# A state-space layer's depthwise convolution: diagonal matrices on TensorE in place of part of VectorE's multiply-adds, with a new split of the C products

## The chip, the cores and the metric

The kernel runs on one core of a Trainium2 chip. The metric is the device time of one execution in microseconds (us); lower is better. TensorE (PE) multiplies matrices, VectorE (DVE), ScalarE (ACT) and GpSimd (POOL) work elementwise, and SyncE (SP) issues nearly all DMAs. Each engine runs its own instructions in order.

## What is computed

Two layers act on eight images of 256 channels and 48x48 pixels, which are 2304 tokens each. Layer 0 normalizes the image by groups, projects it, finds for each token the 16 most similar tokens, and adds their softmax-weighted features. Layer 1 normalizes again and runs two Mamba blocks one after the other. The core of a block, with 512 inner channels, 4 taps of the depthwise convolution and 16 states:

```
xz = x @ in_w.T ;  xi, z = split(xz)
xc = silu(cb + sum_k xpad[:, k:k+L, :] * cw[:, k])       # depthwise convolution, 4 taps
dt_r, Bm, Cm = split(xc @ xp_w.T) ;  dt = softplus(dt_r @ dtp_w.T + dtp_b)
h  = h * exp(dt * A) + dt * Bm * xc                       # scan over the tokens, 16 states
y  = sum_states(h * Cm) + xc * D ;  y = (y * silu(z)) @ out_w.T
```

The changed part is the second line, and where the product `h * Cm` (the "C product") is done.

## The kernel before

**Units.** Each image is cut into six chunks of T = 384 tokens, and each chunk passes two blocks (DEPTH = 2), so an image has 12 units and the program 96. The channels lie in four blocks of 128 (DB = 4). A unit's scan has 16 steps of 32 channels, each with four groups of states side by side on 128 partitions; a step has two parts of two states. So a unit has 32 parts, and the program 3072 scans on DVE.

**The main loop** (L991 to L1008) walks over the parts m. In each part ACT makes the decays of the next part (`decay`, L828, two PSUM buffers), DVE runs the scan (`run_scan`, L843), and POOL makes the inputs B·dt·x two steps ahead (`make_bx`, L804). POOL's C products of the step before come once a step (`pool_part`, L871). Which engine does the C product of a part is set by the letters of `SHARE` (L73): "G" gives it to POOL, "V" to DVE (L845). There are three patterns of 16 letters, used for

- stage 0: units 1 to 9 of an image that has a successor. The next image's top-16 search runs beside them, also on DVE;
- stage 1: units 0, 10 and 11 of such an image. The next image's normalization and projections run beside them;
- stage 2: the last image, which has nothing beside it.

**The rest of a unit** is woven into the loop by two hand-written tables, `between` (emitted before the part's scan) and `behind` (after it). An entry such as `(-21, in_proj, 0)` places `in_proj` of channel block 0 in the part 21 before the unit's first scan. After both, one slice of the next image's attention is emitted (`ahead.go`). The schedule is manual: the order of the tables is each engine's order.

**The convolution before.** `in_proj` (L602) writes a block's 387 columns (three of history and 384 tokens) into PSUM. `tap` (L694, ACT) multiplies by the last tap, adds the bias and writes the tile `xc`. `taps` (L702, DVE) adds the three other taps with one multiply-add each, reading PSUM:

```
nc.vector.scalar_tensor_tensor(
    unit["xc"][e], unit["pe"][e][:, k : k + T], cw[:, unit["d"], e, k : k + 1],
    unit["xc"][e], ALU.mult, ALU.add,
)
```

`silu_x` (L710), `x_proj` (L717), `split`, `step_size` (L732) and `softplus` (L741) follow.

**Buffers.** All matmul outputs but the attention sum share a ring of three PSUM buffers (tag `mm`, L559): a matmul can start only when the third tile before it has been read for the last time. The SBUF tag `ow` has one buffer, used in turn by the squares of the normalization (`square`, L643) and the output weights (`load_out`, L900).

**The start.** Layer 0 of the first image runs alone (L524 to L529). After it, eight 128x128 diagonal matrices of the skip weights `D` are made on DVE (L540) and written to HBM (`diag`); `load_d` fetches them for `sum_states` (L886).

Of the kernel before, what the change touches and what calls it, by code (L numbers as in the profile page):

```python
# [8 lines left out]
F32 = mybir.dt.float32  # L9
BF16 = mybir.dt.bfloat16  # L10
AF = mybir.ActivationFunctionType
ALU = mybir.AluOpType
# [3 lines left out]
P = 128  # L16
# [9 lines left out]
def tile_conv_preact(  # L26
# [18 lines left out]
    nc = tc.nc  # L45
    B, C, N = x.shape
    DEPTH, DI, NS = A_log.shape
    DC = conv_w.shape[2]
# [3 lines left out]
    DB = DI // P  # L52
    NB = N // P
    T = 384
# [3 lines left out]
    G = 32  # L58
# [3 lines left out]
    H = DC - 1  # L62
    PARTS = Q // HQ
# [4 lines left out]
    BLOCK = 16  # L68
    TOPK = (1, 10)
# [3 lines left out]
    SHARE = ("GGVGGGVVGGGGGGVG", "GGGVGVVGVVVGVGVG", "VGVGVGVVGGVVGGVG")  # L73
    assert N % T == 0 and N % P == 0 and T % P == 0 and NS % (J * HQ) == 0

    const = ctx.enter_context(tc.tile_pool(name="const", bufs=1))
    small = ctx.enter_context(tc.tile_pool(name="small", bufs=2))
    hbm = ctx.enter_context(tc.tile_pool(name="hbm", bufs=2, space=DRAM))
# [8 lines left out]
    ident = const.tile([P, P], F32, tag="ident", name="ident")  # L87
# [3 lines left out]
    three = const.tile([P, 1], F32, tag="three", name="three")  # L91
    nc.gpsimd.memset(three, 3.0)
    tiny = const.tile([P, 2], F32, tag="tiny", name="tiny")
# [4 lines left out]
    ones_col = const.tile([P, 1], F32, tag="ones_col", name="ones_col")  # L98
    nc.gpsimd.memset(ones_col, 1.0)
    eps5 = const.tile([P, 1], F32, tag="eps5", name="eps5")  # L100
# [29 lines left out]
    cw = const.tile([P, DEPTH, DB, DC], F32, tag="cw", name="cw")  # L130
    cbias = const.tile([P, DEPTH, DB], F32, tag="cbias", name="cbias")
    dtb = const.tile([P, DEPTH, DB], F32, tag="dtb", name="dtb")
    dpar = const.tile([P, DEPTH, DB], F32, tag="dpar", name="dpar")
# [389 lines left out]

    lefts = [{} for _ in range(B)]  # L524
    with tc.tile_pool(name="first", bufs=1) as pool0, tc.tile_pool(
        name="first_ps", bufs=1, space=PSUM
# [5 lines left out]

    diag = hbm.tile([P, DEPTH, DC + 1, DB, P], F32, tag="diag", name="diag", bufs=1)
    with tc.tile_pool(name="setup", bufs=2) as setup:
        for d in range(DEPTH):
            for t in range(DC, DC + 1):
                dg = setup.tile([P, DB, P], F32, tag="dg", name=f"dg_{d}_{t}")
                for k in range(DB):
                    f = cw[:, d, k, t : t + 1] if t < DC else dpar[:, d, k : k + 1]
                    nc.vector.tensor_scalar(dg[:, k], ident, f, None, ALU.mult)  # L540
                nc.sync.dma_start(diag[:, d, t], dg)

    keep = ctx.enter_context(tc.tile_pool(name="keep", bufs=2))
# [14 lines left out]
    def mm(w, name):  # L558
        return ps.tile([P, 512], F32, tag="mm", name=name, bufs=3)[:, :w]  # L559
# [127 lines left out]
    def load_d(unit, k):  # L687
        unit["dmat"][k] = keep.tile([P, P], F32, tag="dmat", name=f"dmat_{unit['u']}_{k}")
        nc.sync.dma_start(unit["dmat"][k], diag[:, unit["d"], DC, k])

    def tap(unit, e):
        d = unit["d"]
        o = keep.tile([P, T], F32, tag="xc", name=f"xc_{unit['u']}_{e}", bufs=7)
        nc.scalar.activation(  # L694
            o, unit["pe"][e][:, H:], AF.Identity,
            bias=cbias[:, d, e : e + 1], scale=cw[:, d, e, H : H + 1],
        )
        unit["xc"][e] = o

    def taps(unit, e):  # L700
        for k in range(H):
            nc.vector.scalar_tensor_tensor(  # L702
                unit["xc"][e], unit["pe"][e][:, k : k + T], cw[:, unit["d"], e, k : k + 1],
                unit["xc"][e], ALU.mult, ALU.add,
            )
# [86 lines left out]
    def on_pool(unit, i, p):  # L792

        stage = 2 if unit["b"] + 1 == B else 0 if TOPK[0] <= unit["at"] < TOPK[1] else 1
        return SHARE[stage][(i * PARTS + p) % BLOCK] == "G"

# [115 lines left out]
    def leave(unit, cb):  # L912
# [17 lines left out]
        (-35, center), (7, in_proj, 5), (24, sum_states, 2), (-33, variance), (-21, in_proj, 0),  # L930
        (-15, taps, 1), (38, out_proj, 0), (-15, taps, 2), (-14, taps, 3), (-34, square),
        (39, leave, 0), (23, load_rep, "dt", 14), (5, load_rep, "dt", 5), (-4, load_bc, 1), (38, out_proj, 1),
        (17, load_d, 2), (-17, tap, 1), (18, load_rep, "dtx", 13), (-8, times_x, 1), (19, gate, 1),
        (-22, normal), (1, load_rep, "dt", 3), (0, load_rep, "dtx", 4), (15, load_rep, "dt", 10), (6, load_rep, "dtx", 7),
        (10, load_rep, "dtx", 9), (12, load_rep, "dtx", 10), (20, load_rep, "dtx", 14), (11, gate, 0), (-29, spread_root),
        (-19, load_in, 5), (33, load_out), (-22, load_in, 0), (21, load_rep, "dt", 13), (-20, tap, 0),
        (-10, step_size, 1), (9, copy_z, 2), (-18, in_proj, 2), (2, load_rep, "dtx", 5), (10, sum_states, 0),
        (13, load_rep, "dt", 9), (29, gate, 2), (9, silu_z), (7, load_rep, "dt", 6), (19, load_rep, "dt", 12),
        (-6, load_rep, "dtx", 1), (-14, load_in, 7), (-30, root), (9, load_rep, "dt", 7), (4, load_d, 1),
        (-24, load_in, 3), (17, load_rep, "dt", 11), (14, load_rep, "dtx", 11), (-13, x_proj), (-17, load_in, 6),  # L940
        (-3, load_d, 0), (4, load_rep, "dtx", 6), (-4, load_rep, "dtx", 2), (-42, load_v),
    ]
    behind = [
        (-12, split), (-3, load_rep, "dt", 1), (3, in_proj, 4), (-10, step_size, 0), (-5, load_rep, "dt", 0),
        (-8, load_rep, "dtx", 0), (-15, tap, 3), (-1, load_rep, "dt", 2), (-28, scale), (16, load_rep, "dtx", 12),
        (11, load_rep, "dt", 8), (8, in_proj, 6), (17, sum_states, 1), (-14, silu_x), (25, load_rep, "dt", 15),
        (-37, affine), (1, times_x, 2), (7, copy_z, 0), (8, load_rep, "dtx", 8), (-17, tap, 2),
        (-10, softplus), (-16, in_proj, 3), (3, load_rep, "dt", 4), (-29, load_in, 2), (6, in_proj, 7),
        (35, gate, 3), (-2, load_rep, "dtx", 3), (8, copy_z, 1), (40, leave, 1), (-3, times_x, 3),
        (22, load_rep, "dtx", 15), (-16, load_in, 4), (29, load_d, 3), (-37, mean), (-19, taps, 0),  # L950
        (-19, in_proj, 1), (-10, load_bc, 0), (33, sum_states, 3), (-30, root_end), (-9, times_x, 0),
# [39 lines left out]
    for m in range(first, PARTS * NSTEP - HOOKS + last + 1):  # L991
        n, p = divmod(m, PARTS)
# [57 lines left out]
```

## Time and profile before

The time before is 9905.45 us, the median of three runs (9903.67 to 9908.92). The profiled execution spans 9897.1 us. Starts of every 32nd scan in the timeline give the units: the first scan starts at 517.7 us; a unit of stage 0 takes 98.3 us in the mean (63 units), of stage 1 100.5 (21 units), of the last image 89.7 (12 units). The page's first part gives the engines:

| Engine | Busy us | Share of the span | Instructions |
|---|---|---|---|
| PE (matmul) | 8000.3 | 81% | 36736 |
| DVE | 8956.8 | 90% | 7993 |
| ACT | 7322.2 | 74% | 15966 |
| POOL | 8943.3 | 90% | 3927 |

These shares are means over stages with different limits, so they are to be read together with the busy time by stage. A busy matmul row overlaps with its neighbours; its mean duration is not its cost in a stream. The mean granted TensorE clock is 0.889 of full speed, and DMA packets take 44.7% of the 16 DMA engines' time.

### The profile page before, as it was taken

Reading aid. Unit: us, or ns where it says so; the run is one execution under the profiler, and the core shown is the slowest. Engines: PE = TensorE matmul, PEld = TensorE weight load, DVE = VectorE, ACT = ScalarE, POOL = GpSimd, SP = SyncE. Lnnn points to the kernel's source line nnn. Section 1 sums busy time; section 2 is a strip of 40 time slices with the busy share of each in tenths; the row PEclk is TensorE's granted clock in tenths of the full one; section 3 lists DMA queues with packets and bytes.
Section 4 is the critical chain, followed back from the end, with each engine's and each line's share of the span. In section 5 each row is a group of like instructions: output and inputs, shape, how many; then the busy total and the mean of one; then the engine's idle time right before and its main releaser. Section 6 shows DMA issues by size and latency. Waiting matters only on the chain. (4 is left out here: it accounts for less than half of the span.)

```text
span 9897.1 us, 133780 instructions
## 1 busy us (share of the span) xinstructions
PE 8000.3 (81%) x36736; PEld 4388.5 (44%) x36736; DVE 8956.8 (90%) x7993; ACT 7322.2 (74%) x15966; POOL 8943.3 (90%) x3927
## 2 busy tenths in 40 slices
PE   8878887788878888788877888778887788866665
PEld 6644544444534454445444445344544444522222
DVE  4589998999989999899998999899998999988998
ACT  4477777778777877777877787777787778766766
POOL 0099999999989999899998999999998999999999
PEclk9989998899989998899988999889998899977777
DMA  1144445444444444444454444444445444444544
GB/s 32 37 133 126 134 130 152 124 132 129 136 142 131 129 134 137 140 126 133 130 148 128 130 128 134 144 132 125 135 128 152 121 133 127 138 136 129 145 138 122
DMA packets 1243503, 1271.37 MB, mean 128 GB/s; under 512 B 266592, under 2 KB 1215840, under 8 KB 1242752
## 3 DMA queue, kind: packets, MB, share of 16 engines
q1 hardware_dynamic: 1230496, 1262.45, 44.7%
q8 instruction: 293, 4.80, 0.2%
q14 instruction: 458, 3.75, 0.1%
q10 hardware_dynamic: 12256, 0.36, 0.1%
HBM read 1048.94 MB, written 212.86 MB: 127 GB/s over the span
## 5 line engine op out<-in xcount | busy, mean ns | idle before, releaser
L804 POOL TENSOR_TENSOR bx<-BC,dtxr 128x1536 f32<-128x1536 f32 x1536 | 5298.4, 3453 | 115.6 <-PE y L889 59.8
L828 ACT ACTIVATE da<-dtr,A_sb 128x385 f32<-128x385 f32 x6144 | 3591.0, 585 | 871.6 <-DVE bx L843 558.0
L843 DVE TENSOR_TENSOR_SCAN bx<-da,bx 128x770 f32<-128x770 f32 x2040 | 3521.8, 1746 | 190.5 <-ACT da L828 151.4
L871 POOL TENSOR_TENSOR bx<-bx,BC 128x1536 f32<-128x1536 f32 (+1 forms) x1320 | 3303.6, 2503 | 217.5 <-DVE bx L843 205.4
L843 DVE TENSOR_TENSOR_SCAN da<-da,bx 128x770 f32<-128x770 f32 x1032 | 1808.8, 1753 | 193.4 <-ACT da L828 149.0
L602 PE MATMUL pe<-vn,inw 128*128 128x384 f32 (+1 forms) x3072 | 1258.9, 543 | 394.1 <-DVE xr L924 87.0
L399 PE MATMUL psim<-pos 128*128 128x512 f32 (+1 forms) x2880 | 1370.8, 608 | 183.5 <-ACT sim L408 74.7
L465 PE MATMUL po<-feat,aT 128*128 128x256 f32 x5184 | 1364.0, 412 | 13.8 <-ACT aT L454 7.6
L889 PE MATMUL y<-bx,sel 128*32 128x384 f32 x12288 | 1221.2, 533 | 44.2 <-POOL bx L871 37.9
L465 PEld LDWEIGHTS po<-feat,aT 128*128 128x128 f32 x5184 | 1029.8, 205 | 361.9 <-issue 113.9
L845 DVE TENSOR_TENSOR bx<-da,BC 128x768 f32<-128x768 f32 x1032 | 988.8, 958 | 35.5
L602 PEld LDWEIGHTS pe<-vn,inw 128*128 128x128 f32 x3072 | 590.1, 206 | 902.6 <-issue 191.2
L399 PEld LDWEIGHTS psim<-pos 128*128 128x128 f32 x2880 | 552.8, 206 | 818.8 <-issue 470.8
L889 PEld LDWEIGHTS y<-bx,sel 128*32 128x32 f32 x12288 | 394.1, 118 | 856.6 <-issue 725.0
L702 DVE SCALAR_TENSOR_TENSOR xc<-pe,cw,xc 128x384 f32<-128x384 f32 x1152 | 695.7, 611 | 42.8 <-ACT xc L694 15.7
L732 PE MATMUL pd<-dbl,dtp_sb 16*128 16x384 f32 x768 | 424.3, 668 | 342.0 <-ACT dt L741 209.0
L859 ACT COPY h_st<-da 128x2 f32<-128x2 f32 x832 | 131.7, 158 | 686.4 <-DVE bx L845 680.0
L454 ACT ACTIVATE aT<-pt 128x512 f32<-128x512 f32 (+1 forms) x720 | 388.1, 548 | 245.9 <-PE pt L446 239.8
L445 PE MATMUL pt<-ident,sim 128*128 128x128 f32 x2592 | 539.6, 291 | 33.7 <-DVE v L666 17.6
L907 PE MATMUL pw<-z,ow 128*128 128x384 f32 x1536 | 531.5, 499 | 15.0 <-DVE v L666 7.0
L437 ACT ACTIVATE rest<-left,three 128x512 bf16<-128x512 f32 (+1 forms) x720 | 467.0, 670 | 59.7 <-DVE left L422 59.7
L446 PE MATMUL pt<-minus,rest 128*128 128x128 bf16 x2592 | 491.6, 225 | 3.2 <-ACT rest L437 3.2
(146 smaller groups left out, 9766.8 us busy)
## 6 DMA issues: line engine op xcount, KB each, us to landing
dtxr<-dtx_d SPq DMA_DIRECT2D x6144, 48.0 KB, 1.8
dtr<-dt_d SPq DMA_DIRECT2D x6144, 48.0 KB, 1.8
BC<-bc_d SPq DMA_DIRECT2D x768, 192.0 KB, 3.7
inw<-in_in_wT_dram SPq DMA_DIRECT2D x768, 128.0 KB, 2.2
dtx_d<-dtx SPq DMA_DIRECT2D x384, 192.0 KB, 2.0
dt_d<-dt SPq DMA_DIRECT2D x384, 192.0 KB, 2.2
ow<-in_out_wT_dram SPq DMA_DIRECT2D x96, 512.0 KB, 4.0
dmat<-diag SPq DMA_DIRECT2D x384, 64.0 KB, 2.3
```

The source lines that it names most:

```text
L399: nc.tensor.matmul(pm, pos[:, k, t * P : (t + 1) * P], pos[:, k, c0 : c0 + w], start=(k == 0), stop=(k == CB - 1),)
L445: nc.tensor.transpose(pt[:, q], row["sim"][:, r], ident)
L465: nc.tensor.matmul(row["po"], aT[:, m % PT, :], feat[:, m, :], start=(m == 0), stop=(m == NB - 1))
L602: nc.tensor.matmul(pe, w[:, k], unit["vn"][:, k, lo:], start=(k == 0), stop=(k == CB - 1))
L702: nc.vector.scalar_tensor_tensor(unit["xc"][e], unit["pe"][e][:, k : k + T], cw[:, unit["d"], e, k : k + 1], unit["xc"][e], ALU.mult, ALU.add,
L804: nc.gpsimd.tensor_tensor(bx[:, :, 1:], unit["BC"][0], unit["dtxr"][i].unsqueeze(1).to_broadcast([P, Q, T]), ALU.mult,)
L828: nc.scalar.activation(da[:, s * (1 + T) : (s + 1) * (1 + T)], unit["dtr"][i], AF.Exp, scale=A_sb[:, unit["d"], i, p * HQ + s : p * HQ + s ...
L843: nc.vector.tensor_tensor_scan(h, da, g, 0.0, ALU.mult, ALU.add)
L845: nc.vector.tensor_tensor(bx[:, :, 0:T], da.rearrange("p (q t) -> p q t", q=HQ)[:, :, 1:], unit["BC"][1][:, qs], ALU.mult,)
L871: nc.gpsimd.tensor_tensor(g[:, :, 0:T], g[:, :, 1:], unit["BC"][1][:, qs], ALU.mult)
L889: nc.tensor.matmul(y[j * G : (j + 1) * G, :], sel, unit["bx"][k * J + j][:, q, 0:T], start=False, stop=True, skip_group_check=True,)
L907: nc.tensor.matmul(pw, unit["ow"][:, k, cb * P : (cb + 1) * P], unit["z"][k], start=(k == 0), stop=(k == DB - 1),)
```

## The change

For some channel blocks the convolution moves from DVE to PE. A depthwise tap is a product with a diagonal matrix, so four matmuls with the matrices diag(cw[:, k]) against four shifted windows of the block's 387 columns add up the four taps in PSUM. `ON_PE` says for which blocks: 0 and 1 in stage 0, all four in stages 1 and 2. For such a block ACT first copies the 387 columns from PSUM to SBUF (`tap`), PE runs `conv`, and ACT reads the sum back and adds the bias (`drain`); `taps` does nothing. The diagonals, 32 for the taps and 8 for `D`, are made in front of layer 0 of the first image and lie in HBM; `load_taps` fetches those of two blocks (512 KB) into the `ow` buffer.

The time that this frees on DVE goes in part to C products: `SHARE` gives POOL fewer of them, 22 of 32 parts in stage 0 (before 24), 13 of 32 in stages 1 and 2 (before 16). The tables are adapted: `in_proj` of block 1 comes one part earlier, `tap` 1 two parts earlier, `silu_x` and `x_proj` half a part later. Four small constants are put into one tile to save SBUF.

```diff
-    SHARE = ("GGVGGGVVGGGGGGVG", "GGGVGVVGVVVGVGVG", "VGVGVGVVGGVVGGVG")
+    SHARE = ("GGVGGGVVGGGGGGVVGGVGGGVVGGGGGGVV", "GGVVGVVGVVVGVGVGGGVVGVVGVVVGVVVG", "VGVGVGVVGGVVVGVGVGVGVGVVVGVVVGVG")
+    ON_PE = ((0, 1), (0, 1, 2, 3), (0, 1, 2, 3))
...
+    diag = hbm.tile([P, DEPTH, DB, DC + 1, P], F32, tag="diag", name="diag", bufs=1)
+    with tc.tile_pool(name="setup", bufs=2) as setup:
+        for d in range(DEPTH):
+            for k in range(DB):
+                dg = setup.tile([P, DC + 1, P], F32, tag="dg", name=f"dg_{d}_{k}")
+                for t in range(DC + 1):
+                    f = cw[:, d, k, t : t + 1] if t < DC else dpar[:, d, k : k + 1]
+                    nc.vector.tensor_scalar(dg[:, t], ident, f, None, ALU.mult)
+                nc.sync.dma_start(diag[:, d, k], dg)
+
     lefts = [{} for _ in range(B)]
...
     def tap(unit, e):
         d = unit["d"]
-        o = keep.tile([P, T], F32, tag="xc", name=f"xc_{unit['u']}_{e}", bufs=7)
-        nc.scalar.activation(
-            o, unit["pe"][e][:, H:], AF.Identity,
-            bias=cbias[:, d, e : e + 1], scale=cw[:, d, e, H : H + 1],
-        )
-        unit["xc"][e] = o
+        o = keep.tile([P, H + T], F32, tag="xc", name=f"xc_{unit['u']}_{e}", bufs=7)
+        unit["xi"][e], unit["xc"][e] = o, o[:, 0:T]
+        if e in ON_PE[stage(unit)]:
+            nc.scalar.copy(o, unit["pe"][e])
+        else:
+            nc.scalar.activation(
+                o[:, 0:T], unit["pe"][e][:, H:], AF.Identity,
+                bias=cbias[:, d, e : e + 1], scale=cw[:, d, e, H : H + 1],
+            )
...
+    def load_taps(unit, e0):
+        if e0 in ON_PE[stage(unit)]:
+            t = keep.tile([P, DB * C], F32, tag="ow", name=f"cd_{unit['u']}_{e0}", bufs=1)
+            t = t.rearrange("p (e k c) -> p e k c", e=2, k=DC)
+            nc.sync.dma_start(t, diag[:, unit["d"], e0 : e0 + 2, 0:DC])
...
+    def conv(unit, e):
+        if e in ON_PE[stage(unit)]:
+            cv = unit["cv"][e] = mm(T, f"cv_{unit['u']}_{e}")
+            for k in range(DC):
+                nc.tensor.matmul(
+                    cv, unit["taps"][e][:, k], unit["xi"][e][:, k : k + T],
+                    start=(k == 0), stop=(k + 1 == DC),
+                )
+
+    def drain(unit, e):
+        if e in ON_PE[stage(unit)]:
+            nc.scalar.activation(
+                unit["xc"][e], unit["cv"].pop(e), AF.Identity, bias=cbias[:, unit["d"], e : e + 1]
+            )
...
     between = [
+        (-21, in_proj, 0), (-20, tap, 0), (-19, tap, 1), (-18, drain, 0), (-18, in_proj, 2), (-17, drain, 1), (-17, tap, 2),
+        (-15, conv, 2), (-14, conv, 3), (-14, drain, 2), (-13, drain, 3), (-13, silu_x),
...
     behind = [
+        (-20, in_proj, 1), (-19, conv, 0), (-18, conv, 1), (-16, in_proj, 3), (-15, tap, 3), (-25, load_taps, 0),
+        (-17, load_taps, 2), (-13, x_proj), (-12, split), (-3, load_rep, "dt", 1), (3, in_proj, 4), (-10, step_size, 0), (-5, load_rep, "dt", 0),
```

## What the change is predicted to do

> **What bounds the kernel now.** I read the page's first part first: DVE and POOL are both busy 90% of the span, and in the first 440 us POOL has next to nothing to do. So these two come first. The next view is the busy time by stage. I took nine units of stage 0, three of stage 1 and eleven of stage 2 (columns: length; busy us and, in brackets, instructions of PE, PE weight loads, DVE, ACT, POOL; granted clock; DMA share; GB/s):
>
> ```profile
> 1805.00:2688.00 883.00, 762.41 (x3609) 424.23 (x3607) 851.81 (x749) 693.88 (x1519) 864.71 (x323) 0.93 0.46 131
> 2688.00:2991.00 303.00, 222.10 (x986) 118.31 (x985) 257.29 (x241) 216.57 (x473) 266.98 (x171) 0.83 0.49 142
> 8820.00:9806.00 986.00, 606.70 (x2430) 263.91 (x2430) 885.26 (x769) 688.54 (x1516) 921.14 (x384) 0.75 0.48 137
> ```
>
> Per unit, stage 0 is 98.1 us with POOL busy 96.1 (98%) and DVE 94.6 (96%): both are full, and neither alone is the bound. Stage 1 is 101.0 us with POOL 89.0 and DVE 85.8, so some 12 us go to handoffs. Stage 2 is 89.6 us with POOL 83.7 and DVE 80.5. PE fills 86% of stage 0 but 62% of stage 2.
>
> The waits of DVE say what the missing time in stage 2 is (us in total, times, longest):
>
> ```profile
> DVE da L843 <- ACT da L828: 38.1, 17, 3.2
> DVE bx L843 <- ACT da L828: 34.9, 19, 3.1
> ```
>
> That is 6.6 us a unit: a burst on ACT (table load, silu or softplus) makes the next decay late. The same two are 1.4 us a unit in stage 0. The groups by shape give the prices (busy us, mean ns | idle before):
>
> ```profile
> L804 POOL TENSOR_TENSOR bx<-BC,dtxr 128x1536 f32<-128x1536 f32 x1536 | 5298.4, 3453 | 115.6 <-PE y L889 59.8 <-DMA dtxr<-dtx_d 24.6 <-ACT da L828 15.8
> L871 POOL TENSOR_TENSOR bx<-bx,BC 128x1536 f32<-128x1536 f32 x720 | 2292.8, 3184 | 139.2 <-DVE bx L843 131.4 <-DMA xt<-in_x_dram 4.2 <-DVE den L430 2.1
> L871 POOL TENSOR_TENSOR bx<-bx,BC 128x768 f32<-128x768 f32 x600 | 1010.9, 1685 | 78.3 <-DVE bx L843 74.0 <-DMA dtr<-dt_d 3.0 <-DMA dtxr<-dtx_d 0.7
> L845 DVE TENSOR_TENSOR bx<-da,BC 128x768 f32<-128x768 f32 x1032 | 988.8, 958 | 35.5
> L702 DVE SCALAR_TENSOR_TENSOR xc<-pe,cw,xc 128x384 f32<-128x384 f32 x1152 | 695.7, 611 | 42.8 <-ACT xc L694 15.7
> L602 PE MATMUL pe<-vn,inw 128*128 128x387 f32 x1536 | 648.0, 553 | 243.1 <-ACT vn L679 62.8 <-issue 48.6 <-ACT aT L454 30.8
> L907 PE MATMUL pw<-z,ow 128*128 128x384 f32 x1536 | 531.5, 499 | 15.0 <-DVE v L666 7.0 <-DMA ow<-in_out_wT_dram 3.3 <-ACT feat L346 1.3
> L694 ACT ACTIVATE xc<-pe,cbias,cw 128x384 f32<-128x384 f32 x384 | 245.3, 662 | 114.5 <-PE pe L602 114.4
> L337 ACT ACTIVATE pos<-pp,b_pos 128x384 f32<-128x384 f32 x96 | 55.1, 573 | 68.5 <-PE pp L310 68.4
> L761 ACT COPY z<-pe 128x384 f32<-128x384 f32 x288 | 136.7, 475 | 79.2 <-PE pe L602 79.2
> ```
>
> For DVE and PE I use busy over count, since neighbours overlap: a tap costs DVE 695.7/1152 = 0.604 us, and a 384-column matmul in a stream costs PE 0.346 (L907) to 0.422 us (L602), not its 0.5 us of duration.
>
> **What the Trainium skill says.** "Perfetto Trace Analysis", section Identifying the Most-Contended Engine, takes occupancy as a fair measure on Vector and GpSimd and not for matmuls; the trace agrees, as the overlap just used shows. "GPSIMD Engine Reference", section 3.1 Elementwise, gives a two-input fp32 operation on GpSimd 1.96 times its time on Vector; here the 768-wide C product costs 1685 ns against 958, a ratio of 1.76, and I use these. "Perfetto Trace Analysis", section Optimizing Scalar/DVE Operations, warns that the two share an SBUF read port, so that moving work between them may not help; nothing in this trace shows it, as all 1536 POOL products of L804 take 3407 to 3547 ns whatever DVE does. "TensorE: Matmul & The Clock Gate", section Step-by-step, says that weight loads are pulled ahead while the matmuls stay in program order; so a convolution that waits for ACT holds the attention matmuls behind it.
>
> **DVE, part by part.** Blocks on PE: 63 units x 2 + 33 x 4 = 258. Three taps each leave: 774 x 0.604 = -467 us. C products taken from POOL: 63 x 2 + 33 x 3 = 225 x 0.958 = +216 us. Sum -252 us; per unit -3.62 + 1.92 = **-1.71** in stage 0, and -7.25 + 2.87 = **-4.37** in stages 1 and 2.
>
> **POOL.** By the letters, a stage-0 unit loses two products of one part (-3.37 us), a stage-1 unit three (-5.06), a stage-2 unit turns three pairs into single parts (-3 x 1.50 = -4.5). The sum is -372 us. So in stage 0 DVE comes to 92.9 and POOL to 92.7: still level.
>
> **ACT.** Per block a tap of 0.662 becomes a copy of 387 columns, near L761's 0.475, and a drain, near L337's 0.573: +0.386, or +100 us in all, +0.8 a unit in stage 0 and +1.5 elsewhere. ACT is busy 77 of 98 us, and it waits for scans (680 us at L859, 558 at L828 in the whole run), so the busy time itself is hidden. The drain's wait need not be: behind it on ACT stand the next decays, and DVE waits for these. Each drain stands right behind its convolution in the tables (conv 0 after part -19's scan, drain 0 ahead of part -18's). When today's tap waits for its matmul it waits 114.4/73 = 1.57 us. Bounds for the 258 drains are therefore 0 and 405 us of ACT time; as ACT has slack on every part outside its bursts, I take 70 us arriving at DVE.
>
> **PE.** 258 x 4 = 1032 matmuls x 0.346 to 0.422 = +357 to +435 us, about 3.1 us a stage-0 unit: 84.7 becomes 87.8 of some 96 us, 91%. It is hidden if the ring of three PSUM buffers holds. There the change helps: today's projections keep a buffer until DVE's last tap (PE waits 82.4 us for `xc` L702 at the matmul of L886 alone), while on the new path a quick copy frees it. The convolutions add a tile each, emptied one part later.
>
> **DMA.** 63 + 66 = 129 loads of 512 KB, 66 MB on 1271 MB, with 45% of the DMA engines' time in use: hidden. A load of this size takes 4.0 us to land (that of the output weights); blocks 2 and 3 have from the end of part -17 to part -15, some 3 to 5 us, so PE may wait 1 to 2 us there in stages 1 and 2, where over a quarter of its time is free. The `ow` buffer's wait stops the SP queue for part of a part, and the replica loads behind it run one to two steps ahead.
>
> **The start loses.** Before, the image loads go out at once. ACT and DVE there (start us, duration):
>
> ```profile
> 4.82 1.02 DVE L261 BATCH_NORM_STATS2 st<-xs 128x6 f32<-128x384 f32 x2 [4.82 <-DMA xs<-in_x_dram]
> ...
> 27.87 0.23 DVE L155 TENSOR_SCALAR A_sb<-A_sb 128x128 f32<-128x128 f32 x1 [11.58 <-ACT A_sb L153]
> ```
>
> Layer 0's statistics end at 16 us, and ACT takes their mean at 24.0, after its own DMA issues. In the changed program's order, all eight diagonal writes stand ahead of the image loads on SP, which also reuse the space of their tiles; and on DVE the last two sets stand behind L155. So: 28.1 + 10 x 0.28 (L540 took 0.28 each) = 31; the write lands 2.5 later; the load takes 4.0, the statistics 11: they end near 48.6 instead of 16, and the mean comes near 49 instead of 24: +25 us, with nothing beside it. At the end of the lone stage, the old setup held the load of `v` from 442 to 445: -3. Net **+22** (10 to 28).
>
> **The sum.** Stage 0: both full engines lose 1.7 and 3.4, so 63 x 1.71 = -108 if the idle share stays. Stage 1: units that lose 12 us to handoffs won't follow DVE in full; 60% of 21 x 4.37 is -55. Stage 2: 12 x 4.37 = -52, as ACT's bursts stay what they are. New drain waits +70, but POOL's relief and the looser ring give back part of DVE's 3.5 idle us in stage 0, for which I take 1.1 x 63 = -70. With the start +22: -193, hence **9712 us**.
>
> **Rivals.**
> - *PE becomes the bound of stage 0*: at 91% it pays for each added matmul, so stage 0 gains nothing; half of stages 1 and 2 (-72) and the start: 9855. For it speaks PE's 86%; against it, that PE's longest waits there are for ACT.
> - *The drain's wait replaces the taps*: two thirds of 405 us reach DVE, +270, with the same -252 and +22: 9945, slower. For it: the short distance of conv and drain, and 1.4 to 6.6 us a unit that DVE already waits for decays. Against: ACT's waits for scans.
> - *Everything follows*: stage 0 gains POOL's full 3.37, the others 4.37: -212 - 144 + 22 gives 9571.
>
> **How the numbers follow.** The sum as computed 0.60, spread over 9630 to 9810; PE bound 0.14, mostly 9810 to 9900; drain waits 0.13; everything follows 0.13, half of it under 9620. A range of 9620 to 9900 leaves out the drain rival and half of the last, 0.2. Faster by over 0.2% (under 9886): 0.60 + 0.13 + 0.09 = 0.82; within 0.2%: 0.05; slower: 0.13.
>
> **What would show it.** Right: DVE down by some 250 us and POOL by 370 in the first part, PE up by 400; stage-0 units near 96 us, stage 2 near 86; the first statistics about 30 us late. The drain rival would show as ACT waiting over 200 us on the convolution's rows and DVE's waits for L828's decays doubled; the PE rival as PE over 95% in stage 0 with DVE under 93%. I am wrong if DVE's busy time falls as computed and the units don't get shorter.

## The result and the profile after

The changed kernel takes **10558.1 us** (median, 10550.2 to 10569.2) against 9907.0 us of the kernel before (9903.7 to 9908.9) on the same chip: a ratio of 1.0658, 95% interval 1.0640 to 1.0677. The forecast was 9712 us, faster; it was wrong in direction and by 846 us. The profiled execution spans 10550.1 us at a mean granted clock of 0.892 (before 0.889), so the clock is no part of it.

The page's first part, to be read against the table of engines of before:

```profile
PE 8642.9 (82%) x38800; PEld 4798.1 (45%) x38800; DVE 8738.7 (83%) x7476; ACT 7435.5 (70%) x16254; POOL 8590.9 (81%) x3738
```

DVE is busy for 218 us less than before and POOL for 352 us less: the work did leave them. PE is busy for 643 us more. Every share but PE's fell. So no engine became full; all of them wait more.

The busy time by stage (nine units of stage 0, three of stage 1, eleven of the last image; columns as in the prediction):

```profile
1916.00:2860.00 944.00, 821.02 (x3759) 459.87 (x3758) 826.90 (x698) 698.28 (x1528) 830.72 (x303) 0.92 0.45 127
2860.00:3192.00 332.00, 247.19 (x1078) 134.74 (x1079) 257.76 (x230) 226.18 (x496) 259.36 (x165) 0.84 0.49 141
9428.00:10457.00 1029.00, 694.20 (x2788) 321.49 (x2792) 842.41 (x670) 707.95 (x1591) 875.00 (x385) 0.80 0.50 143
```

Per unit of stage 0, DVE is busy 91.9 us (826.90/9; before 94.6) and POOL 92.3 (before 96.1), as forecast, but PE 91.2 (before 84.7), and the unit takes 104.9 us: DVE's idle time went from 3.5 to 13 us.

What DVE waits for, over the whole run (us in total, times, longest). First before:

```profile
DVE bx L843 <- ACT da L828: 151.4, 186, 3.1
DVE da L843 <- ACT da L828: 149.0, 61, 5.7
DVE z L895 <- PE y L889: 117.7, 69, 4.3
...
DVE xr L491 <- PE pr L482: 13.4, 2, 12.3
```

Then after (L843 is now L873, L828 is L858, L895 is L925, L491 is L490):

```profile
DVE bx L873 <- ACT da L858: 386.4, 158, 6.6
DVE da L873 <- ACT da L858: 316.8, 169, 6.5
DVE xr L490 <- PE pr L481: 286.8, 65, 12.3
DVE z L925 <- PE y L919: 275.4, 100, 7.2
```

These four rows hold most of the answer. Scans waiting for decays went from 300 to 703 us: that is ACT being late. The last step of the attention (`xr` waits for the transposed sum `pr`) went from 13 to 287 us, and the gate (`z` waits for `sum_states`) from 118 to 275 us: that is PE being late. POOL feels it too: its next inputs go into buffers that `sum_states` must have read, and they wait for that 287 us in all, against 60 before. The groups by shape give the work that was added and removed (busy us, mean ns | idle before):

```profile
L726 PE MATMUL cv<-xc,cd 128*128 128x384 f32 x2064 | 735.1, 500 | 69.3 <-DMA cd<-diag 54.2 <-ACT xc L698 8.7 <-ACT da L858 5.4
L709 DVE SCALAR_TENSOR_TENSOR xc<-pe,cw,xc 128x384 f32<-128x384 f32 x378 | 230.8, 611 | 16.6 <-ACT xc L700 7.7
L733 ACT ACTIVATE xc<-cv,cbias 128x384 f32<-128x384 f32 x258 | 148.9, 577 | 375.4 <-PE cv L726 375.2
L698 ACT COPY xc<-pe 128x387 f32<-128x387 f32 x258 | 121.8, 472 | 2.9 <-PE pe L601 2.9
```

The first line shows an error of the prediction at sight: the program has 258 x 4 = 1032 convolution matmuls, and the trace has 2064 rows (instructions that the trace lists). The drains wait 375 us for their convolutions.

### The profile page after: what moved, and what is told of

Read it like the earlier page. It is cut to its first block, busy times and chain, and to the rows that moved or that the text cites. A ratio compares the mean times of both kernels' runs of the same rounds, so it can differ in the third digit from the quotient of the medians.

```text
span 10550.1 us, 137600 instructions
## 1 busy us (share of the span) xinstructions
PE 8642.9 (82%) x38800; PEld 4798.1 (45%) x38800; DVE 8738.7 (83%) x7476; ACT 7435.5 (70%) x16254; POOL 8590.9 (81%) x3738
## 4 chain that ended last, share of the span: by engine, by line
DVE 36%; PE 24%; ACT 19%; issue 8%; DMA 6%; SPq 6%; POOL 2%; ACTq 0%; POOLq 0%; DVEq 0%
DVE da L873 11%; DVE bx L873 10%; ACT da L858 7%; PE cv L726 6%; SPq L575 4%; PE pe L601 4%; DVE bx L875 3%; PE po L464 3%; DVE top L414 3%; PE psim L398 3%; DVE left L417 2%; PE y L919 2%; DMA dtxr<-dtx_d 2%; DVE xc L709 2%; PE px L747 1%
## 5 line engine op out<-in xcount | busy, mean ns | idle before, releaser
L858 ACT ACTIVATE da<-dtr,A_sb 128x385 f32<-128x385 f32 x6144 | 3590.9, 585 | 783.4 <-DVE bx L873 437.3
L901 POOL TENSOR_TENSOR bx<-bx,BC 128x768 f32<-128x768 f32 (+1 forms) x1131 | 2928.8, 2590 | 723.1 <-DVE bx L873 444.1
L873 DVE TENSOR_TENSOR_SCAN bx<-da,bx 128x770 f32<-128x770 f32 x1815 | 3134.8, 1747 | 407.4 <-ACT da L858 386.4
L873 DVE TENSOR_TENSOR_SCAN da<-da,bx 128x770 f32<-128x770 f32 x1257 | 2204.3, 1754 | 343.4 <-ACT da L858 316.8
L398 PE MATMUL psim<-pos 128*128 128x512 f32 (+1 forms) x2880 | 1381.7, 617 | 161.7 <-DVE xc L709 104.3
L601 PE MATMUL pe<-vn,inw 128*128 128x384 f32 (+1 forms) x3072 | 1206.5, 523 | 285.2 <-DVE xr L954 88.1
L875 DVE TENSOR_TENSOR bx<-da,BC 128x768 f32<-128x768 f32 x1257 | 1204.3, 958 | 43.2
L919 PE MATMUL y<-bx,sel 128*32 128x384 f32 x12288 | 1178.4, 521 | 26.4 <-DVE bx L875 23.1
L726 PE MATMUL cv<-xc,cd 128*128 128x384 f32 x2064 | 735.1, 500 | 69.3 <-DMA cd<-diag 54.2
L747 PE MATMUL px<-xc,xp_sb 128*48 128x384 f32 x768 | 368.7, 639 | 283.1 <-ACT xc L740 283.1
L762 PE MATMUL pd<-dbl,dtp_sb 16*128 16x384 f32 x768 | 385.6, 618 | 260.6 <-ACT dt L771 211.7
L726 PEld LDWEIGHTS cv<-xc,cd 128*128 128x128 f32 x2064 | 396.8, 195 | 371.6 <-issue 33.0
```

What stands on the lines that cost most here:

```text
L398: nc.tensor.matmul(pm, pos[:, k, t * P : (t + 1) * P], pos[:, k, c0 : c0 + w], start=(k == 0), stop=(k == CB - 1),)
L601: nc.tensor.matmul(pe, w[:, k], unit["vn"][:, k, lo:], start=(k == 0), stop=(k == CB - 1))
L726: nc.tensor.matmul(cv, unit["taps"][e][:, k], unit["xi"][e][:, k : k + T], start=(k == 0), stop=(k + 1 == DC),)
L858: nc.scalar.activation(da[:, s * (1 + T) : (s + 1) * (1 + T)], unit["dtr"][i], AF.Exp, scale=A_sb[:, unit["d"], i, p * HQ + s : p * HQ + s ...
L873: nc.vector.tensor_tensor_scan(h, da, g, 0.0, ALU.mult, ALU.add)
L875: nc.vector.tensor_tensor(bx[:, :, 0:T], da.rearrange("p (q t) -> p q t", q=HQ)[:, :, 1:], unit["BC"][1][:, qs], ALU.mult,)
```

## The experiments

Unit means are taken as for the kernel before, from the starts of every 32nd scan. Every kernel was timed beside the kernel before on the same chip; differences with a plus sign are against that timing of it (medians of 9898 to 9907 us).

| Kernel | us (median) | Ratio (95% interval) | Unit: stage 0 / 1 / last image |
|---|---|---|---|
| before | 9907.0 | 1 | 98.3 / 100.5 / 89.7 |
| the change | 10558.1 | 1.0658 (1.0640 to 1.0677) | 105.6 / 106.4 / 93.5 |
| none_on_pe | 10390.2 | 1.0499 (1.0468 to 1.0529) | 103.3 / 105.7 / 94.4 |
| old_share | 10483.4 | 1.0593 (1.0562 to 1.0623) | 104.3 / 106.4 / 93.6 |
| one_tap | 10174.7 | 1.0281 (1.0245 to 1.0316) | 101.8 / 101.6 / 90.0 |
| pe_load_here | 10143.7 | 1.0249 (1.0220 to 1.0279) | 101.8 / 101.5 / 89.3 |
| pe_load_spread | 10072.8 | 1.0176 (1.0133 to 1.0220) | 100.9 / 101.1 / 89.3 |
| share_only | 10027.8 | 1.0131 (1.0087 to 1.0174) | 99.6 / 101.0 / 92.0 |
| order_only | 10284.9 | 1.0391 (1.0346 to 1.0435) | 102.4 / 104.5 / 92.5 |
| silu_back | 9936.0 | 1.0035 (1.0021 to 1.0050) | 98.8 / 100.2 / 89.7 |
| silu_alone | 9945.0 | 1.0037 (1.0017 to 1.0057) | 98.9 / 100.7 / 89.8 |
| x_proj_later | 10227.2 | 1.0329 (1.0299 to 1.0359) | 102.3 / 102.1 / 92.2 |
| change_silu_back | 10376.0 | 1.0479 (1.0451 to 1.0510) | 102.5 / 105.8 / 96.0 |
| last_image | 10016.4 | 1.0116 (1.0087 to 1.0146) | 98.8 / 100.7 / 96.4 |
| last_once | 9969.4 | 1.0069 (1.0046 to 1.0092) | 98.8 / 100.7 / 92.2 |
| last_once_sum | 9974.1 | 1.0076 (1.0047 to 1.0105) | 99.3 / 101.1 / 89.7 |
| last_two | 9916.8 | 1.0017 (1.0009 to 1.0025) | 98.9 / 100.4 / 88.9 |
| last_two_letters | 9900.3 | 1.0000 (0.9990 to 1.0010) | 98.9 / 100.4 / 87.2 |
| rows_by_image | 9874.0 | 0.9972 (0.9961 to 0.9982) | 98.3 / 101.0 / 87.3 |
| four_by_image | 9889.1 | 0.9987 (0.9980 to 0.9994) | 98.3 / 100.7 / 88.3 |

### Which part of the change costs the time

**none_on_pe** leaves the new rows, letters and setup, with no block on PE:

```diff
-    ON_PE = ((0, 1), (0, 1, 2, 3), (0, 1, 2, 3))
+    ON_PE = ((), (), ())
```

> The changed kernel with no channel block on TensorE: tables, split of the C products and early setup stay, only the convolutions go back to VectorE. Three theories. P (TensorE's queue): the convolution costs TensorE two passes per matmul, 735 us in all, in a stretch where its queue was full, and VectorE waits behind. Then all of the excess but the start's goes, and VectorE, with 216 us of C products more than before, sets the time: 9905 + 23 for the start + 120 to 200, about 10,050 to 10,130 us. H (handoff): the drains' waits on ScalarE delay the decays; the same is expected, 10,050 to 10,130. S (split and order): the new split of the C products and the new order of the tables cost the time; then it stays over 10,400 us.

10390 us, just under the bound of S: still 5% slower than before without a single convolution on PE. So most of the loss needs neither the convolution on PE nor its handoffs.

**old_share** puts the old letters into the changed kernel (`SHARE` as before, the rest as changed).

> The changed kernel with the old split of the C products (24, 16 and 16 of 32 parts on GpSimd). P: stage 0 is set by TensorE and doesn't care, since neither VectorE (2 us less a unit) nor GpSimd (3.4 us more, 96 of 105) is the bound: within 0.7% of 10,558 us. H: VectorE's time still counts beside the waits, so its 216 us less show at least by half: 10,350 to 10,450. S: most of the loss is undone, under 10,250 us.

75 us faster than the change, at the edge of P's range and short of H's. POOL again has its C products and DVE loses 216 us of them: the letters are a smaller part.

**one_tap** keeps copies, loads, drains, letters and rows, and runs one matmul of each convolution's four; three of four taps are left out for those blocks:

```diff
-            for k in range(DC):
+            for k in range(DC - 1, DC):
...
-                    start=(k == 0), stop=(k + 1 == DC),
+                    start=True, stop=True,
```

> The changed kernel with one matmul per block in place of four: three of the four taps are left out on the blocks that TensorE convolves. Copy, wait, drain, loads and order stay, so all handoffs are there; TensorE's added passes fall from 2064 to 516. P: the loss goes nearly whole: VectorE at 93 and GpSimd at 93 us set stage-0 units of 95 to 98 us, and the time is 9,750 to 9,950 us. H: the drains and the waits stay, so most of the loss stays: over 10,300 us.

383 us faster than the change, between the two forecasts, so the amount of work on PE matters, with all handoffs in place. DVE's wait for `pr` falls from 287 to 76 us and that for `sum_states` from 275 to 191.

**order_only** is the work of before in the new order: no block on PE and the old letters, with the new rows and the setup in front.

> The changed kernel with no block on TensorE and the old split of the C products: every engine has the work of the kernel before, only the order of the tables and the early setup are the new ones. The runs so far left 10,390 us with nothing on TensorE, so a fourth theory, O (order), stands beside P and S: the new rows put x_proj on TensorE directly behind silu_x of ScalarE, in front of the part's attention matmuls instead of behind them, and TensorE's whole queue waits there for silu_x. O: 10,150 to 10,330 us. S (split): the order is harmless, 9,910 to 9,980 us.

10285 us: **+382 us from the order and the setup alone**, the largest single part. The letters, added to that, give none_on_pe (+105 us), and the convolution on PE, added to that, the change (+168 us, although it takes 467 us of taps from DVE).

### The row of silu_x

**silu_back** is order_only with two rows, `silu_x` and `x_proj`, put where they were; **silu_alone** moves back `silu_x` only, **x_proj_later** puts `x_proj` half a part later still and leaves `silu_x` in its new place:

```diff
-        (-15, conv, 2), (-14, conv, 3), (-14, drain, 2), (-13, drain, 3), (-13, silu_x),
+        (-15, conv, 2), (-14, conv, 3), (-14, drain, 2), (-13, drain, 3),
...
-        (-17, load_taps, 2), (-13, x_proj), (-12, split), ...
+        (-17, load_taps, 2), (-12, split), ...
...
+        (-13, x_proj)          # in between
+        (-14, silu_x)          # in behind
```

> order_only with silu_x and x_proj put back to their old rows (silu_x behind part -14, x_proj in front of part -13's scan); the other moved rows (in_proj 1, tap 0 to 2 and the place of the rows in their parts) stay. O with silu_x and x_proj as the cause: back to the kernel before plus the start's 10 to 15 us, 9,900 to 9,980. If another moved row is the cause: as order_only, within 60 us.

> order_only (10,285 us) with silu_x alone put back behind part -14; x_proj keeps its new row behind part -13. Two theories of the 349 us between order_only and silu_back. R (ScalarE's own wait): in the old row ScalarE runs the silu burst in time in which it would wait for VectorE's scan of part -14; one part later it first idles there (3.3 us in the last image) and then makes the next decays wait behind the burst. Q (TensorE's queue): x_proj now waits for silu_x with the attention matmuls behind it. R: 9,920 to 9,990 us. Q: with silu_x early, x_proj does not wait either, so the same is expected; the next run tells them apart.

> order_only with x_proj alone half a part later (in front of part -12's scan, behind the attention matmuls of part -13); silu_x keeps its new row. Q: TensorE no longer waits with attention behind it, so most of the 349 us go: under 10,050 us. R: the burst still stands behind ScalarE's wait, and split comes yet closer to x_proj: 10,230 to 10,340 us.

silu_back takes away 349 of the 382 us, silu_alone 340, x_proj_later 58. One row, moved by half a part, costs 3.4% of the run. DVE's waits for decays in order_only:

```profile
DVE bx L873 <- ACT da L858: 374.9, 157, 4.4
DVE da L873 <- ACT da L858: 224.7, 110, 6.7
```

and in silu_back:

```profile
DVE da L873 <- ACT da L858: 147.8, 62, 5.6
DVE bx L873 <- ACT da L858: 142.1, 186, 3.1
```

600 against 290 us: the 310 us are most of the difference in time. The timeline shows how. ACT in silu_back, around part -14 of unit 88 (start us, us, then in brackets the idle time before and what ended it):

```profile
9178.66 1.21 ACT L858 ACTIVATE da<-dtr,A_sb 128x385 f32<-128x385 f32 x2 [3.25 <-DVE bx L873]
9179.89 1.28 ACT L738 ACT_TABLE_LOAD   x1
9181.18 1.76 ACT L740 ACTIVATE xc<-xc 128x384 f32<-128x384 f32 x4
9182.96 1.28 ACT L741 ACT_TABLE_LOAD   x1
9184.25 0.16 ACT L889 COPY h_st<-da 128x2 f32<-128x2 f32 x1
9184.44 1.20 ACT L858 ACTIVATE da<-dtr,A_sb 128x385 f32<-128x385 f32 x2
```

and the same stretch in order_only, ACT first, then the two scans of DVE that follow:

```profile
9504.84 1.20 ACT L858 ACTIVATE da<-dtr,A_sb 128x385 f32<-128x385 f32 x2 [3.25 <-DVE bx L873]
9509.32 0.16 ACT L889 COPY h_st<-da 128x2 f32<-128x2 f32 x1 [3.28 <-DVE bx L875]
9509.52 1.20 ACT L858 ACTIVATE da<-dtr,A_sb 128x385 f32<-128x385 f32 x2
9510.66 0.18 ACT L911 COPY h_st<-bx 128x2 f32<-128x2 f32 x1
9510.84 1.28 ACT L738 ACT_TABLE_LOAD   x1
9512.13 1.76 ACT L740 ACTIVATE xc<-xc 128x384 f32<-128x384 f32 x4
9513.91 1.28 ACT L741 ACT_TABLE_LOAD   x1
9515.21 1.21 ACT L858 ACTIVATE da<-dtr,A_sb 128x385 f32<-128x385 f32 x2
```

```profile
9516.45 1.76 DVE L873 TENSOR_TENSOR_SCAN bx<-da,bx 128x770 f32<-128x770 f32 x1 [2.37 <-ACT da L858]
9519.24 1.77 DVE L873 TENSOR_TENSOR_SCAN da<-da,bx 128x770 f32<-128x770 f32 x1 [1.03 <-ACT da L858]
```

The burst is the same 4.35 us in both. In the old row it runs while ACT would wait anyway: the copy of the last state (`h_st`) needs DVE's scan and C product. Half a part later that copy stands ahead of the burst. ACT first idles 3.28 us, then copies, makes one decay, and only then starts the burst; the decay of the next part comes 4.35 us late, and DVE stands still for 2.37 and 1.03 us.

The table loads take the 1283 ns that the Trainium skill gives in "ScalarE: Activation LUTs", section What ACT_TABLE_LOAD costs; the 1380 ns of draining that it adds to each doesn't show here, as the next activation starts within 0.02 us.

The rival was that the loss is PE's wait for `silu_x` (at `px`, 331 us in order_only against 29 in silu_back), with the attention's matmuls queued behind it. x_proj_later doesn't settle this alone: its `px` still waits 320 us, because half a part later is still behind the burst, and its waits for decays are still 595 us. The timeline does for this unit: the decay that ends the 2.37 us stands right behind the burst on ACT and needs nothing of PE. Only the second gap, 1.03 us, is ended by a decay that stood behind a copy which waited 0.97 us for `px`. For the whole run the sums of all waits do. DVE waits for PE 237 us in silu_back, 273 in order_only and 224 in x_proj_later, and ACT 931, 986 and 940. So in x_proj_later they wait hardly longer for PE than in silu_back, and still 291 of the 349 us are lost: the rival can have little more than the 58 us that came back.

**change_silu_back** puts `silu_x` and `x_proj` back in the whole change, with convolution 3 and its drain just ahead of it.

> The whole change with the order mended: silu_x behind part -14 and x_proj in front of part -13's scan as before; for this drain 3 stands right ahead of silu_x and conv 3 behind part -15, right behind tap 3. If the costs add, 10,558 - 349 = 10,210 us. If TensorE's full stretch is what is left (stage-0 units near 101.8 us as in pe_load_here, stages 1 and 2 with their gain of 2 to 4 us a unit), 10,050 to 10,150 us. If the order was all, the blind forecast's 9,712 holds: under 9,800 us.

182 us faster than the change, not 340, and slower than all three forecasts. DVE's waits for decays fall from 703 to 505 us. Stage 0 stops at 102.5 us a unit, where something else now holds it. The wait for `pr` has not moved:

```profile
DVE xr L490 <- PE pr L481: 286.3, 65, 12.3
```

### The load on PE

**pe_load_here** adds to the kernel before, in stage-0 units alone, the change's eight matmuls where the convolutions stand, with a result that nobody reads; **pe_load_spread** puts the same eight at eight different parts:

```diff
+    def load_pe(unit, n):
+        if unit["b"] + 1 < B and TOPK[0] <= unit["at"] < TOPK[1]:
+            t = mm(T, f"load_{unit['u']}")
+            for k in range(n):
+                nc.tensor.matmul(t, ident, unit["vn"][:, 0, k : k + T], start=(k == 0), stop=(k + 1 == n))
...
+        (-19, load_pe, 4), (-18, load_pe, 4),
```

> The kernel before with eight more 384-column fp32 matmuls in each stage-0 unit, four behind part -19 and four behind part -18, where the convolutions of the changed kernel stand. Their result is read by nobody, so there is no copy, no drain, no load and no change in the split. P: 63 units x 8 x 2 passes x 0.36 us = 363 us more on TensorE in a full stretch: stage-0 units get 4 to 7 us longer, 10,150 to 10,350 us. H: without a handoff little happens: 9,900 to 9,980 us.

> The kernel before with the same eight added matmuls per stage-0 unit as in pe_load_here, which took 10,144 us, but one at a time behind parts -21, -17, -13, -9, -5, -1, 3 and 7. If TensorE's load over the whole unit is the bound, the place is nothing: within 60 us of 10,144. If it is the full stretch around part -19, most of the 246 us go: under 10,000 us.

+246 us, 6 us short of P's range, and +170, between its two forecasts. In pe_load_here no ACT, no DMA and no reader is involved: matmuls alone lengthen stage 0 by 3.5 us a unit. The wait that grows is the one seen after the change:

```profile
DVE xr L491 <- PE pr L482: 228.8, 51, 12.3
```

229 us where it was 13, nearly the whole 246. It belongs to the place: in pe_load_spread, with the same eight matmuls, it is back at 13.4 us. There the loss shows elsewhere: DVE waits 187 us for `sum_states` (before 118), and POOL waits 172 us for it (before 60). But pe_load_spread is not a test of the amount alone, because each of its eight matmuls takes a buffer of the ring of three for itself and waits until ACT has read an earlier tile:

```profile
L718 PE MATMUL load<-vn,ident 128*128 128x384 f32 x1008 | 530.3, 613 | 185.7 <-ACT vo L926 75.7 <-ACT sim L408 65.8 <-ACT z L767 35.2
```

In pe_load_here the added matmuls wait 5.7 us in all. So how the 2.6 us a unit of pe_load_spread divide between PE's time and the ring stays open.

In the changed kernel, PE in that stretch of a stage-0 unit:

```profile
2163.77 1.47 PE L601 MATMUL pe<-vn,inw 128*128 128x387 f32 x4
2165.07 2.74 PE L726 MATMUL cv<-xc,cd 128*128 128x384 f32 x8
2167.66 1.88 PE L398 MATMUL psim<-pos 128*128 128x512 f32 x4
2169.37 1.47 PE L601 MATMUL pe<-vn,inw 128*128 128x387 f32 x4
2170.67 2.74 PE L726 MATMUL cv<-xc,cd 128*128 128x384 f32 x8
2173.26 0.38 PE L481 MATMUL pr<-ident,o 128*128 128x128 f32 x2
```

and DVE at its end:

```profile
2173.67 0.35 DVE L490 SCALAR_TENSOR_TENSOR xr<-pr,b_feat,xr 128x128 f32<-128x128 f32 x1 [4.47 <-PE pr L481]
```

PE has no gap for ten microseconds; the small `pr` stands behind two convolutions, and DVE, whose next scan stands behind `xr`, waits 4.47 us. change_silu_back's 102.5 us a unit is close to pe_load_here's 101.8, and its wait for `pr` is that of the change: once `silu_x` is back, this is most of what stage 0 pays.

A convolution is 8 rows for four matmuls, 2.74 us. Over the run the 2064 rows occupy PE for 735.1 us, 0.356 a row and 0.712 a matmul. Of this the end of a convolution's last row overlaps with what follows: in the listing above the next work starts 2.59 us after the start of the convolution, 0.65 us a matmul. The Trainium skill, "FP8 and Floating Point Precision", section TensorE Precision Notes, has true fp32 as four passes through the array. The Trainium skill, "TensorE: Matmul & The Clock Gate", section Back-to-back issue gap, gives N/2.4 + 2.5 ns for one isolated matmul of N columns at full clock. Taken once per pass, this is an estimate of 0.65 us for 384 columns, which agrees with the 0.65 of this listing.

### The letters alone

**share_only** is the kernel before with the new `SHARE` (indexed by its own length).

> The kernel before with the new split of the C products and nothing else: VectorE has 216 us more, GpSimd 372 us less. S: over 10,200 us. Else VectorE's time shows in part: stage 0 was level between VectorE and GpSimd, stages 1 and 2 had slack, so 9,960 to 10,110 us.

+125 us: with 225 C products more on DVE and its taps still there, a unit takes 99.6 us in stage 0 and 92.0 in the last image (before 98.3 and 89.7). In old_share the reverse is worth 75.

### The last image

Here no attention runs and PE has time, so this is where the convolution on PE should pay. **last_image** has all four blocks on PE in the last image only, the old letters in stages 0 and 1, the old rows of `silu_x` and `x_proj`, and the setup woven into layer 0 of the first image.

> A version meant to beat both: the order of change_silu_back, TensorE convolves in the last image alone (all four blocks, with the new split there), stages 0 and 1 have the work and the split of the kernel before, and the diagonals are made beside layer 0 of the first image, behind its loads. Stages 0 and 1 then cost as in silu_back, without its later start. TensorE has 38% to spare in the last image: 12 units x 2 to 4 us less gives 9,855 to 9,895 us. If drains and loads still hold ScalarE up there, 9,905 to 9,950 us.

96.4 us a unit, worse than the change itself (93.5) and as in change_silu_back (96.0); both forecasts were missed. Two suspects: the diagonals of blocks 2 and 3 come late, because the `ow` buffer is free only after convolution 1, and 34 rows of `sum_states` (17 matmuls in the program; the forecasts below count the rows) stand ahead of convolution 3. Four kernels take these apart: **last_once** loads all 32 diagonals once, into a buffer that is idle in the last image; **last_once_sum** also moves `sum_states` 1 one part later; **last_two** leaves blocks 2 and 3 on DVE; **last_two_letters** has the old letters as well.

```diff
-                t = keep.tile([P, DB * C], F32, tag="ow", name=f"cd_{unit['u']}_{e0}", bufs=1)
+                t = keep.tile([P, CB, N], F32, tag="pos", name="cd_all", bufs=1)      # last_once: one load in all
...
-        (17, sum_states, 1)
+        (18, sum_states, 1)                                                             # last_once_sum
...
-    ON_PE = ((), (), (0, 1, 2, 3))
+    ON_PE = ((), (), (0, 1))                                                            # last_two
```

> As last_image, all four blocks on TensorE in the last image, but the 32 diagonals of both Mamba blocks are loaded once, into the buffer of the positional features, which nothing uses in the last image. Late-load theory: the 2.6 to 3.0 us for which convolution 2 waits for its load go, and with them 2 to 4 of the 6.7 us that a unit of the last image lost: 92.5 to 94.5 us a unit, 9,970 to 9,995. Rival (the load is hidden behind the wait for sum_states and the drains): within 10 us of 10,016.

> As last_once, with sum_states of block 1 of the unit before moved one part later, so that its 34 matmuls stand behind convolution 3 and not ahead of it. Late-load theory with the queue on TensorE: convolution 3 starts at once, drain 3 and silu wait no longer, and a unit of the last image takes 88 to 91 us, 9,885 to 9,940. Rival (the drains and the burst on ACT cost by themselves): 93 us or more, above 9,960.

> As the kernel last_image (old rows of silu_x and x_proj, old letters in stages 0 and 1, new letters in the last image, setup beside layer 0), but in the last image only blocks 0 and 1 are convolved on TensorE. Late-load theory (the last image lost because the diagonals of blocks 2 and 3 come late through the one ow buffer and convolution 3 stands behind 34 matmuls of sum_states): both causes are gone, so a unit of the last image takes 89 to 91 us instead of 96.4, and the time is 9,890 to 9,940. Amount theory (each block on TensorE costs about the same): half the loss stays, 93 us a unit, 9,960 to 9,990.

> As last_two, with the old letters in the last image too, so POOL keeps its 16 C products of 32 and DVE loses six taps (3.6 us of its 80.5) with nothing in return. If C products are worth more on DVE than on POOL there, this is slower than last_two by up to 3 x 1.5 = 4.5 us a unit (50 us). If neither engine bounds the last image, both agree within 15 us. If the convolution on TensorE is worth anything, a unit takes less than 89 us and the time is under 9,890.

The late load costs 96.4 - 92.2 = 4.2 us a unit, the place of `sum_states` 2.5 more; then four blocks on PE are level with before (89.7). The drains' waits, in the last image's stretch, follow: last_image, last_once, last_once_sum:

```profile
ACT xc L729 <- PE cv L722: 104.2, 40, 5.6
```

```profile
ACT xc L734 <- PE cv L727: 54.9, 24, 4.4
```

```profile
ACT xc L734 <- PE cv L727: 24.2, 25, 1.4
```

As a whole last_once_sum missed its 9,885 to 9,940: the row of `sum_states` moved in every stage, and the first seven images lost 0.4 to 0.6 us a unit against last_once, some 44 us, against 12 x 2.5 = 30 gained in the last. Two blocks give 88.9 us and with the old letters 87.2, 2.5 below before: the first clear gain, and the new letters cost 1.7 us a unit here. But as a whole last_two_letters is level with before, since stage 0 is 0.6 us a unit longer without any block on PE. In silu_back, with nearly the same rows, DVE's wait for `pr` came 57 times and 30 us, against 2 and 13.

**rows_by_image** gives the new rows to the units of the last image only; **four_by_image** does the same for the kernel last_once_sum, that is for all four blocks, but with the old letters:

```diff
-        for table, rows in ((inner, between), (outer, behind)):
+        last_image = unit["b"] + 1 == B
+        rows_in, rows_out = (between, behind) if last_image else (between_old, behind_old)
+        for table, rows in ((inner, rows_in), (outer, rows_out)):
```

> As last_two_letters (blocks 0 and 1 of the last image on TensorE, all letters as before), but the units of the first seven images keep the rows of the kernel before and only the last image's units have the new ones. If the new rows alone cost the first seven images their 0.6 us a unit in stage 0 (98.9 against 98.3), that comes back: 98.3, 100.5 and 87.2 us a unit, so 12 x 2.5 = 30 us faster than before, 9,865 to 9,880. If the 2.5 us of the last image came from the run of the stages ahead of it, the time is 9,890 to 9,905.

> As last_once_sum in the last image (all four blocks on TensorE, diagonals loaded once, sum_states of block 1 one part later), with the letters of before there, and with the rows of before in the first seven images. If the last image's remaining cost is the amount of work on TensorE and ACT (four copies, drains and 32 matmul passes more), a unit takes 89 to 90 us there: 9,895 to 9,915. If it is the C products that the letters moved to DVE (last_two against last_two_letters: 1.7 us a unit), it takes 87 to 88: 9,865 to 9,885.

rows_by_image takes 9874 us, 26 us faster than before (ratio 0.9972, 0.9961 to 0.9982), and is the only version that beats it by more than 0.2%. The rows alone don't make this gain: silu_back, with nearly the same rows and nothing on PE, has 89.7 us a unit in the last image. In rows_by_image the wait for `pr` is back at that of before:

```profile
DVE xr L490 <- PE pr L481: 13.4, 2, 12.3
```

Four blocks do no better than two (88.3 against 87.3 us a unit). The time of four_by_image fell between its two forecasts: the old letters are worth 1.4 us a unit against last_once_sum (89.7), and 1.0 remains above two blocks. That the added work on PE and ACT costs this 1.0 is likely but not shown, as the row of `sum_states` and the load differ, too.

## Why the prediction was wrong, point by point

- **DVE, POOL and ACT busy time: right.** Forecast -252, -372 and +100 us; measured -218, -352 and +113. Stage 0's 92.9 and 92.7 us a unit came out as 91.9 and 92.3. But the step from busy time to unit length ("if the idle share stays") failed: the prediction's own test, busy time down and units not shorter, is what happened.
- **The moved rows: the step that failed most.** `silu_x` and `x_proj` half a part later were in the diff and in no term of the sum. They were costed at nothing with no work named that hides them. order_only measured 382 us with the setup, of which 340 are `silu_x`: the decay behind its burst comes 4.35 us late, and DVE's waits for decays grow by some 300 us. The prediction had read the mechanism off the profile (a burst on ACT makes the next decay late, 6.6 us a unit in stage 2) and then took the bursts to "stay what they are".
- **PE: the term mis-sized by a factor of two.** 1032 matmuls at 0.346 to 0.422 us gave +357 to +435 us; it was 735. The time per row was right (0.356), but rows were taken for matmuls. (PE's busy time as a whole rose by less, 643 us, as neighbouring rows overlap.) The rows of L907 in the prediction's own listing could have told: 96 units x 2 output blocks x 4 input blocks are 768 matmuls, and it shows x1536. So the convolutions of a stage-0 unit take not 3.1 us but 5.7 (8 matmuls x 0.712), and PE's 84.7 us became 91.2.
- **"Hidden if the ring holds": wrong in kind.** The rival "PE becomes the bound" was given 0.14 and was to cost no more than stage 0's gain. PE is at 87% of the stage-0 stretch, not over 95%, and 88% (806/912) in pe_load_here, and still the matmuls added there cost 246 us. What they delay is what stands behind them in PE's order: `pr`, and through DVE's order the next scan. The shares of the engines didn't show this; the program order did.
- **The drains: mechanism seen, evidence misjudged.** Their waits came to 375 us, close to the upper bound of 405. The prediction's sign for this rival, ACT waiting over 200 us on the convolution and DVE's waits for decays doubled, came true in full. Yet none_on_pe has no drains, and its waits for decays are 346 + 226 = 572 of the change's 703 us: the row of `silu_x` doubles them by itself. With that row back, change_silu_back still has 505 us of them against 300 before, and its drains wait 438 us for their convolutions: so the drains probably cost as well, but no run leaves out the drains alone. A sign that two causes share tells neither.
- **DMA "hidden": wrong in the last image.** PE was to wait 1 to 2 us in time that it had free. In the order of last_image, loading once was worth 4.2 us a unit there.
- **The start: right in size, but by luck.** Forecast +22, measured 540.3 - 517.7 = +22.6 us for the first scan, but by another way: the first statistics begin at 27.4 us instead of 4.8 and end at 37.2, not 48.6, and the first normalization is only 14 us late. The rest arises ahead of the first scan, and 13 us of it only with blocks on PE (none_on_pe's first scan starts at 527.2). last_image, with the setup woven into layer 0, starts at 517.7 again.
- **POOL's relief and the looser ring** (-70 us) don't show: DVE's idle time in stage 0 rose from 3.5 to 13 us. PE's waits for DVE's last tap, which the ring was to ease, were 119 us in the whole run (82 of them at the skip matmul of `sum_states`) and are 104 after, now in front of the attention's `psim`.

The parts don't add: `silu_x` costs 340 us alone and 182 in the whole change, since with `silu_x` back PE's load still holds stage 0 near 102 us a unit. What stays open is how the 5.9 us of stage 1 in the change divide: order_only alone has 4.0 of them, yet change_silu_back gives only 0.6 back and one_tap 4.8. The matmuls, the late load and the drains probably replace what the row cost, and no run takes them apart in that stage.

## What to carry to other kernels

In a hand-ordered schedule every moved row is a part of the change with a cost of its own: ask what stands behind it on its engine, and in which wait it was hidden; here half a part for a 4.35 us burst cost 340 us. Before work goes to an engine "with room", count what one of its operations is in the trace (rows against calls in the source), and look for the short operation that will stand behind it there and that another engine needs at once; run the old work in the new order first, which separates the two. And put new work only where the stage has time for it: the same convolution on two blocks gained 2.4 us a unit in the last image, and its rows alone lost 0.6 elsewhere.

## What was not expected of the hardware

An fp32 matmul of 384 columns is two rows of the trace and occupies PE for 0.712 us (735.1/1032), 0.65 from start to start in a stream, with one weight load per row (2064, 396.8 us busy beside it). Matmuls that nobody reads, and that waited 5.7 us in all, lengthen a stage in which PE was busy for 86% of the time by 3.5 us a unit for 5.6 us of added work (352.7/63); DVE's wait for one short matmul behind them grew by 215 of the 246 us.
